# Moving the load of x from SyncE's queue to ScalarE's in a state-space and attention kernel

## The chip, the cores and the metric

The kernel runs on one core of a Trainium2 chip. A core has five engines that work side by side: TensorE (PE, matmuls), VectorE (DVE), ScalarE (ACT), GpSimd (POOL) and SyncE (SP), which here only issues DMAs. Each engine takes its instructions strictly in the order in which they were written, and that includes the instructions that issue DMAs: an instruction that has to wait holds up everything behind it on its engine. The metric is the time of one execution in device microseconds (us). Before the change it is 10996.49 us, the median of three runs (10985.81 to 11037.44).

## The reference

The input is x of 16 images with 128 channels and 64 x 64 pixels, that is 4096 tokens each, in float32. There are two layers.

```python
x = x + mamba(group_norm(x))          # layer 0
t = tokens(x)
t = t + attention(layer_norm(t))      # layer 1
t = t + moe(layer_norm(t))
```

Layer 0 is a selective state-space block: `xz = u @ W_in` gives 256 inner channels and a gate z; a causal convolution of width 4 and a silu follow; a projection gives dt, B and C; and for each of 16 states n the recurrence `h = exp(delta * A_n) * h + delta * u * B_n` runs over the tokens, with `y = sum over n of C_n * h`. Then `y * silu(z)` is projected back with `W_out` and added to x. The attention is a causal running softmax with eight fixed queries (a running maximum, a running sum and a running weighted sum of values). The mixture of experts lets each of 64 experts choose eight tokens, pools them, applies two matrices and adds the result back.

## The kernel before

The kernel has three phases: layer 0 and the attention of layer 1 interleaved (to about 10,150 us, nearly everything); the choice of tokens for the experts; the experts and the last sum. The change touches only the first.

The first phase cuts each image into 8 blocks of L = 512 tokens, 128 blocks in all, with channels on the partitions. The main loop runs over k, the number of the block, and inside it over n, the number of the state, 0 to 15. Everything is put into that double loop by hand: the order of the source is the order on each engine, since every engine is wrapped in `InOrder`, whose one line (L31) is why nearly all rows of the profile bear the line L31. Rows are told apart by the names of their tiles.

In step (k, n) VectorE makes the product `bx` of `du` with B_n (`product`) and runs two scans (`scan`) that give h; POOL multiplies h by C_n into `da` and, for each odd n below 14, issues a DMA that adds the previous state's `da` to this one (`add_pair`); TensorE turns such sums of pairs into PSUM tile `y_ps` (`add_y`). At n = 4 `add_y` takes states 0 and 1. B_n and C_n of a block come to all partitions in one load of tile `bct`, 512 KB, issued by SP in `load_bc` three states ahead, from a small DRAM tile `bcs`. There are five buffers of `bct`, so the load for state n waits until POOL has finished state n - 5.

The rest of the work of several blocks is written between these steps in `beside(n)` and `between(n)`. With m = k - 9 the block that the attention works on, and k + 1 the next block:

- n = 1 to 3: `norm_block` normalises the x of block k + 1 in place (ScalarE). `turn_y` turns the y of block k - 1 back into `yb_ps`, and `gate` (n = 3, VectorE) multiplies it by the gate `z`.
- n = 7: ScalarE stores the attention's split scores to DRAM (`pd<-parts`, `store_parts`).
- n = 8: TensorE projects block k + 1 (`dbl_ps`), and ScalarE stores its B and C (`bcs<-dbl`, `store_bc`).
- n = 9: `gate_silu` of block k: two matmuls `z_ps` read the x tile `xb` of block k, and two silus on ScalarE make `z`. Then come four value matmuls `v_ps` and their silus.
- n = 10: `delta` of block k + 1 (`dt_ps`, softplus on ScalarE), the variance and `rstd` of the attention's next block.
- n = 12, 13: `weights` reads `lh` and `rh` (`w_ps`); `attend` makes `ao_ps`.
- n = 14: VectorE makes the attention's input `xn` from `cen_ps` and `rstd`, right after the product of that state.

The tile `xb` of a block holds its 512 tokens and the three before them, which the convolution needs; the first block of an image has zeros there, put in by a memset on POOL. There are two buffers of `xb`, so the load for block k + 2 overwrites that of block k, whose last readers are the two `z_ps` matmuls of n = 9.

In SP's queue the order around the change, after `load_bc` of state 13 (issued at n = 10), is: the load of `xb` for block k + 2; 16 small loads of 3 KB each that spread `pd` into `lh` and `rh` (`spread_parts`); the load of `bct` for state 14 (issued at n = 11), that for state 15 (n = 12), a load of `xs` from DRAM (`load_x`), and so on.

Of the kernel before, what the change touches and what calls it, by code (L numbers as in the profile page):

```python
# [16 lines left out]
L = 512  # L17
# [22 lines left out]
def conv_attn_hybrid(ctx: ExitStack, tc: tile.TileContext, x, w_in, conv_w, conv_b, w_xproj, w_dt, b_dt,  # L40
# [4 lines left out]
    NBLK = T // L  # L45
# [6 lines left out]
    KC = conv_w.shape[1]  # L52
# [8 lines left out]
    x_f = x.rearrange("b c h w -> b c (h w)")  # L61
# [19 lines left out]
    with ExitStack() as st:  # L81
# [5 lines left out]
        PE, DVE, ACT, POOL, SP = (InOrder(tc, e) for e in (nc.tensor, nc.vector, nc.scalar, nc.gpsimd, nc.sync))  # L87
# [127 lines left out]
        NK = NB * NBLK  # L215
        blocks, gn, res, att = {}, {}, {}, {}

        def load_exp():
            tc.keep_in_program_order(nc.scalar.preload_act_table_set(EXP_LN))
# [4 lines left out]
        def bank(name):  # L224
            return ps.tile([P, L], F32, tag="ps", name=name)
# [13 lines left out]
        def gn_stats(b, i):  # L239
            DVE.bn_stats(gn[b]["stats"][:, i, :], gn[b]["t"])  # L240

        def gn_end(b, part):

            w = gn[b]
            if part == 0:
                w["mv"] = stp.tile([P, 2], F32, tag="mv", name="mv")
                w["gs"] = stp.tile([P, 5], F32, tag="gs", name="gs")
                DVE.bn_aggr(w["mv"], w["stats"].rearrange("p a b -> p (a b)"))
            mv, gs = w["mv"], w["gs"]
            if part == 1:  # L250
                w["gp"] = bank("gn_ps")
                PE.matmul(w["gp"][:, 0:1], gmat, mv[:, 0:1], start=True, stop=True)
                ACT.copy(gs[:, 0:1], w["gp"][:, 0:1])
            if part == 2:
                DVE.tensor_tensor(gs[:, 1:2], mv[:, 0:1], gs[:, 0:1], ALU.subtract)
                DVE.scalar_tensor_tensor(gs[:, 1:2], gs[:, 1:2], gs[:, 1:2], mv[:, 1:2], ALU.mult, ALU.add)
            if part == 3:
                w["gp"] = bank("gn_ps2")
                PE.matmul(w["gp"][:, 0:1], gmat, gs[:, 1:2], start=True, stop=True)
                ACT.activation(gs[:, 2:3], w["gp"][:, 0:1], AF.Ln, bias=eps)  # L260
                ACT.activation(gs[:, 3:4], gs[:, 2:3], AF.Exp, scale=-0.5)
            if part == 4:
                DVE.tensor_scalar(gs[:, 4:5], gs[:, 0:1], gs[:, 3:4], -1.0, ALU.mult, ALU.mult)


        def load_block(k):

            b, i = divmod(k, NBLK)
            t = xbp.tile([P, KC - 1 + L], F32, tag="xb", name="xb")
            if i == 0:  # L270
                POOL.memset(t[:, : KC - 1], 0.0)
                SP.dma_start(t[:, KC - 1 :], x_f[b, :, :L])
            else:
                SP.dma_start(t, x_f[b, :, i * L - (KC - 1) : (i + 1) * L])
            blocks[k] = dict(k=k, b=b, i=i, xb=t)

        def norm_block(k):
            w = blocks[k]
            t, gs = w["xb"], gn[w["b"]]["gs"]
            t = t[:, KC - 1 :] if w["i"] == 0 else t  # L280
            ACT.activation(t, t, AF.Identity, bias=gs[:, 4:5], scale=gs[:, 3:4])
# [14 lines left out]
        def gate_silu(k):  # L296
            w = blocks[k]
            z = w["z"] = m1.tile([P, NH2, L], F32, tag="z", name="z")
            for a in range(NH2):
                pt = bank("z_ps")  # L300
                PE.matmul(pt, wz[:, bass.ts(a, P)], w["xb"][:, KC - 1 :], start=True, stop=True)
                ACT.activation(z[:, a, :], pt, AF.Silu)
# [36 lines left out]
        def load_bc(k, n):  # L339
            w = blocks[k]  # L340
            t = w["bc", n] = bcp.tile([P, 2, L], F32, tag="bc", name="bct")
            SP.dma_start(t, w["bcs"][n : n + N + 1 : N, :].partition_broadcast(P))
# [7 lines left out]
        def product(k, n):  # L350

            w = blocks[k]
            bx = w["bx"] = bps.tile([P, NH2, L], F32, tag="bx", name="bx")
            DVE.tensor_tensor(bx, w["du"], bc(w["bc", n][:, 0:1, :], [P, NH2, L]), ALU.mult)
# [17 lines left out]
        def add_pair(k, n):  # L372

            w = blocks[k]
            POOL.dma_start(w["da", n], w.pop(("da", n - 1)), accum_op=ALU.add)

        def keep_state(k, n):
            w = blocks[k]
            h = w.pop(("h", n))
            if w["i"] < NBLK - 1:  # L380
                POOL.tensor_copy(gn[w["b"]]["state"][:, n, :], h[:, :, L - 1])
# [53 lines left out]
        def store_residual(b, part):  # L435
            SP.dma_start(t1_d[b, :, bass.ts(part, T // 4)], res[b][:, bass.ts(part, T // 4)])
# [15 lines left out]
        def ln_center(m):  # L452
            s = att[m]
            s["cen"] = bank("cen_ps")
            PE.matmul(s["cen"], cmat, s.pop("x"), start=True, stop=True)

        def ln_square(m):
            s = att[m]
            s["sq"] = short("sq")
            ACT.activation(s["sq"], s["cen"], AF.Square)  # L460
# [131 lines left out]
        def value(m, c, g):  # L592
            s = att[m]
            if g == 0:
                s["v", c] = vp_.tile([P, HD, P], F32, tag="v", name="v")
            hs = bass.ts(g, 4)
            vp = ps.tile([P, 4, P], F32, tag="ps", name="v_ps")
            PE.matmul(vp.rearrange("p h d -> p (h d)"), s["xn"][:, bass.ts(c, P)],
                      wv[:, hs, :].rearrange("p h d -> p (h d)"), start=True, stop=True)
            ACT.activation(s["v", c][:, hs, :], vp, AF.Silu)  # L600
# [72 lines left out]
        def decays(k, n, count, lead=LEAD):  # L673

            nonlocal made
            for _ in range(count):
                if made < len(order) and made <= k * N + n + lead and order[made][0] in blocks \
                        and "delta" in blocks[order[made][0]]:
                    decay(*order[made])
                    made += 1  # L680
# [4 lines left out]
        for i in range(2):  # L685
            gn_load(1, i)
            gn_stats(1, i)
        load_block(0)
        load_block(1)
        load_exp()  # L690
        for part in range(5):
            gn_end(0, part)
# [13 lines left out]
        for k in range(NK + LAG + 1):  # L706
            b, i = divmod(k, NBLK)
# [22 lines left out]
            def beside(n):  # L730
# [104 lines left out]
                if n == 9:  # L835
                    if mn is not None:
                        ln_center(mn)
                        ln_square(mn)
                    if cur is not None:
                        gate_silu(cur)  # L840
                    if m is not None:
                        value(m, 1, 0), value(m, 1, 1)
                if n == 10:
# [30 lines left out]
            for n in range(N):  # L874
                if cur is not None:
                    product(cur, n)
                if ends is not None and n == 2:
                    gn_end(ends, 0)
                beside(n)
                if n in (4, 11, 12, 15):  # L880
                    decays(k, n, 2)
                if cur is not None:
                    later = k * N + n + LEAD_BC
                    if later < NK * N:
                        load_bc(*order[later])
                    scan(cur, n, between)
                    keep_state(cur, n)
                    if n % 2 and n < N - 2:
                        add_pair(cur, n)
                else:  # L890
                    between(n)
                if cur is not None and n >= 4 and n % 2 == 0:
                    add_y(cur, n - 3)

                if 8 <= n <= 11 and i == 0 and prev is not None:
                    store_residual(b - 1, n - 8)
                if 14 <= n <= 15 and i == 0 and cur is not None:
                    load_residual(b, n - 14)
                if n < 2 and i == 1 and cur is not None:
                    load_residual(b, n + 2)  # L900
                if n == 7 and mn is not None:
                    load_x(mn, True)
                if n == 8 and stat is not None:
                    gn_load(*stat)
                if n == 10 and k + 2 < NK:
                    load_block(k + 2)
                if n == 10 and m is not None:
                    spread_parts(m)
                if n == 12 and m is not None:
                    load_x(m)  # L910
# [8 lines left out]
    with ExitStack() as st:  # L919
        PE, DVE, ACT, POOL, SP = (InOrder(tc, e) for e in (nc.tensor, nc.vector, nc.scalar, nc.gpsimd, nc.sync))  # L920
# [163 lines left out]
        for it in range(NIT + LATE + 2):  # L1084
            p, i = divmod(it, NBLK)
# [73 lines left out]
    with ExitStack() as st:  # L1159
        ps = st.enter_context(tc.tile_pool(name="cps", bufs=4, space=PSUM))  # L1160
        cp = st.enter_context(tc.tile_pool(name="cp", bufs=2))
        for pr in range(NB // 2):
# [4 lines left out]
            for j in range(2):  # L1167
                b = 2 * pr + j
                t = cp.tile([P, T], F32, tag=f"t{j}", name=f"tc{j}")
# [34 lines left out]
```

## Time and profile before

| | |
|---|---|
| median of three runs | 10996.49 us |
| the profiled execution | 11003.26 us |
| its span | 11001.4 us |
| TensorE busy | 9347.4 us (85%), mean granted clock 0.894 |
| VectorE busy | 8982.2 us (82%) |
| ScalarE busy | 7293.5 us (66%) |
| POOL busy | 7464.0 us (68%) |
| blocks 10 to 126, mean time of one | 76.3 us |
| blocks 0 to 8 (no attention yet), mean time of one | 64.6 us |

A row of the groups reads: line, engine, operation, tile written <- tiles read, shape, count | busy us in all, mean ns of one | idle time of the engine just ahead of these instructions, and what ended it. In the waits, a row reads: the engine and the tile that it was about to write, <- what it waited for, then us in total, times, and the longest. SPq and ACTq are the DMA-issuing instructions of SP and ScalarE. The idle time of an engine costs something only if the work that ends the block hangs on it.

### The profile page before, as it was taken

How to read it: one execution, taken by the hardware profiler on the slowest of the kernel's cores; microseconds unless marked ns; L12 is line 12 of the kernel's file. 1: busy time of each engine (PE TensorE's matmuls, PEld its weight loads, DVE VectorE, ACT ScalarE, POOL GpSimd, SP SyncE). 2: the span in 40 equal slices, each digit the busy share in tenths (PEclk: the TensorE clock that was granted, in tenths of full speed). 3: DMA queues.
4: the chain of work that ended last, by engine and by line, in shares of the span. 5: the costliest groups of instructions: out<-in, count | busy, mean ns of one | idle time of the engine just before them, and what ended most of it. 6: DMA issues, size and time to landing. Idle time of an engine off the chain costs nothing.

```text
span 11001.4 us, 157987 instructions
## 1 busy us (share of the span) xinstructions
PE 9347.4 (85%) x55389; PEld 5527.2 (50%) x55389; DVE 8982.2 (82%) x9987; ACT 7293.5 (66%) x12924; POOL 7464.0 (68%) x4771
## 2 busy tenths in 40 slices
PE   4578888888888889998888888988888888888775
PEld 2345555555555555555555555555545555544652
DVE  8998888888889888888888888888888888830753
ACT  5567677776777767777676776777767777754740
POOL 7887777777777777777777777777777777720000
PEclk7789999999999999999999999999999999999886
DMA  7777777777777777777777777777767777720348
GB/s 191 199 198 180 193 181 193 181 194 180 180 200 180 192 178 195 183 196 179 182 188 179 196 181 192 182 198 183 192 176 182 198 180 189 178 71 29 113 158 336
DMA packets 944361, 1995.67 MB, mean 181 GB/s; under 512 B 103040, under 2 KB 188688, under 8 KB 936400
## 3 DMA queue, kind: packets, MB, share of 16 engines
q1 hardware_dynamic: 751056, 1448.08, 45.0%
q0 software_dynamic: 129024, 469.82, 21.9%
q10 hardware_dynamic: 63488, 67.67, 1.8%
q8 instruction: 440, 7.21, 0.2%
q14 instruction: 353, 2.89, 0.1%
HBM read 1363.98 MB, written 151.52 MB: 138 GB/s over the span
## 4 chain that ended last, share of the span: by engine, by line
PE 53%; ACT 15%; DVE 14%; DMA 9%; issue 6%; SPq 2%; POOL 1%; ACTq 1%; DVEq 0%; POOLq 0%
PE ao_ps L31 9%; PE xs_ps L31 7%; DVE h L31 6%; PE v_ps L31 6%; PE y_ps L31 5%; DMA da<-da 5%; PE k_ps L31 5%; DVE bx L31 4%; PE o_ps L31 4%; ACT da L31 4%; PE carry_ps L31 4%; PE dbl_ps L31 2%; DMA bct<-bcs 2%; ACT wm L31 2%; SPq L31 2%
## 5 line engine op out<-in xcount | busy, mean ns | idle before, releaser
L31 POOL TENSOR_TENSOR da<-h,bct 128x1024 f32<-128x1024 f32 x2048 | 6454.8, 3152 | 2069.6 <-DVE h L31 1635.8
L31 DVE TENSOR_TENSOR_SCAN h<-da,state,bx 128x512 f32<-128x512 f32 x3584 | 4414.5, 1265 | 170.0 <-DVE bx L31 2.9
L31 DVE TENSOR_TENSOR bx<-du,bct 128x1024 f32<-128x1024 f32 x2048 | 2590.6, 1265 | 882.0 <-DMA bct<-bcs 816.3
L31 ACT ACTIVATE da<-delta,a_neg 128x512 f32<-128x512 f32 x4096 | 2629.5, 716 | 107.3 <-DMA da<-da 87.8
L31 PE MATMUL y_ps<-ident,da 128*128 128x128 f32 x9216 | 1415.6, 307 | 381.4 <-DMA da<-da 381.1
L31 PEld LDWEIGHTS y_ps<-ident,da 128*128 128x128 f32 x9216 | 1198.4, 159 | 817.9 <-DMA da<-da 437.8
L31 PE MATMUL ao_ps<-wm,v 128*128 128x128 f32 x8192 | 1259.7, 317 | 239.0 <-ACT wm L31 195.4
L31 PEld LDWEIGHTS ao_ps<-wm,v 128*128 128x128 f32 x8192 | 1186.5, 227 | 503.8 <-ACT wm L31 320.6
L31 PE MATMUL v_ps<-wv,xn 128*128 128x512 f32 x2048 | 1060.3, 640 | 261.1 <-ACT xc L31 241.3
L31 ACT ACTIVATE v<-v_ps 128x512 f32<-128x512 f32 x1024 | 610.1, 597 | 733.0 <-PE v_ps L31 731.1
L31 ACT ACTIVATE wm<-w_ps 128x512 f32<-128x512 f32 x1024 | 552.4, 591 | 708.7 <-PE w_ps L31 707.2
L31 PE MATMUL k_ps<-xn,wk 128*128 128x512 f32 x2048 | 946.7, 596 | 5.6 <-ACT kt L31 5.3
L31 PE MATMUL xs_ps<-xb,wc 128*128 128x512 f32 x2048 | 925.2, 594 | 1.8 <-issue 1.8
L31 POOL DMA_DIRECT2D da<-da x896 | 788.0, 879 | 172.2 <-POOL state L31 98.1
L31 PEld LDWEIGHTS v_ps<-wv,xn 128*128 128x128 f32 x2048 | 346.9, 195 | 784.1 <-issue 301.5
L31 ACT ACTIVATE kt<-k_ps 128x512 f32<-128x512 f32 x1024 | 585.9, 600 | 180.5 <-PE k_ps L31 151.8
L31 DVE TENSOR_TENSOR_SCAN h<-da,bx 128x512 f32<-128x512 f32 x512 | 599.8, 1206 | 25.6 <-ACT da L31 0.5
L31 PEld LDWEIGHTS xs_ps<-xb,wc 128*128 128x128 f32 x2048 | 371.1, 191 | 397.9 <-issue 383.3
L31 ACT ACT_TABLE_LOAD x395 | 506.8, 1283 | 52.0 <-ACT parts L31 46.3
L31 PEld LDWEIGHTS k_ps<-xn,wk 128*128 128x128 f32 x2048 | 371.4, 191 | 328.8 <-issue 254.2
L31 POOL COPY state<-h 128x2 f32<-128x2 f32 x1792 | 461.7, 258 | 0.0
L31 PE MATMUL w_ps<-rh,lh 64*128 64x512 bf16 x1024 | 293.9, 431 | 183.4 <-DMA rh<-pd 83.9
(196 smaller groups left out, 10704.8 us busy)
## 6 DMA issues: line engine op xcount, KB each, us to landing
bct<-bcs SPq DMA_DIRECT2D x2048, 512.0 KB
da<-da POOLq DMA_DIRECT2D x896, 512.0 KB, 7.6
xs<-t_d SPq DMA_DIRECT2D x240, 256.0 KB
xs<-in_x_dram SPq DMA_DIRECT2D x128, 256.0 KB
xt<-in_x_dram SPq DMA_DIRECT2D x64, 512.0 KB
t_d<-xt SPq DMA_DIRECT2D x64, 512.0 KB
t_d<-xs ACTq DMA_DIRECT2D x256, 128.0 KB
t<-t_d SPq DMA_DIRECT2D x128, 256.0 KB
```

The source lines that it names most:

```text
L31: return lambda *args, **kw: self.tc.keep_in_program_order(f(*args, **kw))
```

## The change

`load_block` gets the queue as an argument. The two loads ahead of the loop stay on SP. In the loop the load for block k + 2 is now issued by ScalarE at n = 9, right behind the two silus of `gate_silu` and ahead of the silus of v, instead of by SP at n = 10 behind `load_bc` of state 13 and ahead of the spread loads. The memset of the three columns for the first block of an image, 16 in all, is split off into `no_tokens`; it stays on POOL and goes from n = 10 to n = 13.

```diff
-        def load_block(k):
+        def load_block(k, queue):
 
             b, i = divmod(k, NBLK)
             t = xbp.tile([P, KC - 1 + L], F32, tag="xb", name="xb")
             if i == 0:
-                POOL.memset(t[:, : KC - 1], 0.0)
-                SP.dma_start(t[:, KC - 1 :], x_f[b, :, :L])
+                queue.dma_start(t[:, KC - 1 :], x_f[b, :, :L])
             else:
-                SP.dma_start(t, x_f[b, :, i * L - (KC - 1) : (i + 1) * L])
+                queue.dma_start(t, x_f[b, :, i * L - (KC - 1) : (i + 1) * L])
             blocks[k] = dict(k=k, b=b, i=i, xb=t)
+
+        def no_tokens(k):
+            if k % NBLK == 0:
+                POOL.memset(blocks[k]["xb"][:, : KC - 1], 0.0)
...
-        load_block(0)
-        load_block(1)
+        for k in range(2):
+            load_block(k, SP)
+            no_tokens(k)
...
                     if cur is not None:
                         gate_silu(cur)
+                    if k + 2 < NK:
+                        load_block(k + 2, ACT)
                     if m is not None:
                         value(m, 1, 0), value(m, 1, 1)
...
-                if n == 10 and k + 2 < NK:
-                    load_block(k + 2)
+                if n == 13 and k + 2 < NK:
+                    no_tokens(k + 2)
                 if n == 10 and m is not None:
                     spread_parts(m)
```

## The prediction

> **What bounds the kernel now.** I read the page first, then the waits of the DMA queue of SP, then one block in order of time, then the waits of TensorE over the steady stretch, and last the stretches of one block with their clock.
>
> The page (engine totals, then two groups: busy, mean ns | idle before, releaser):
>
> ```profile
> span 11001.4 us, 157987 instructions
> PE 9347.4 (85%) x55389; PEld 5527.2 (50%) x55389; DVE 8982.2 (82%) x9987; ACT 7293.5 (66%) x12924; POOL 7464.0 (68%) x4771
> ...
> L31 DVE TENSOR_TENSOR bx<-du,bct 128x1024 f32<-128x1024 f32 x2048 | 2590.6, 1265 | 882.0 <-DMA bct<-bcs 816.3
> ...
> L31 PE MATMUL y_ps<-ident,da 128*128 128x128 f32 x9216 | 1415.6, 307 | 381.4 <-DMA da<-da 381.1
> ```
>
> VectorE loses 816 us to loads of B and C (`bct`). The waits of SP's queue (waited for: us, times, longest) say which wait in front of those loads is not simply a full buffer:
>
> ```profile
> SPq L31 <- POOL state L31: 4850.8, 1218, 8.3
> SPq L31 <- POOL da L31: 1456.0, 308, 8.2
> SPq L31 <- PE z_ps L31: 1063.1, 118, 12.8
> ```
>
> The POOL rows are free buffers being awaited, well ahead of need. The z_ps row is the load of x: 118 times 9.0 us. One block in order of time (start, duration; four lines of SP's queue, the third of them the first of 16 spread loads, then one of VectorE):
>
> ```profile
> 5019.47 0.36 SPq L31 DMA_DIRECT2D bct<-bcs  x1
> 5029.72 0.35 SPq L31 DMA_DIRECT2D xb<-in_x_dram  x1
> 5030.15 0.27 SPq L31 DMA_DIRECT2D lh<-pd  x1
> ...
> 5036.94 0.89 SPq L31 DMA_DIRECT2D bct<-bcs  x2
> 5042.63 1.23 DVE L31 TENSOR_TENSOR bx<-du,bct 128x1024 f32<-128x1024 f32 x1 [7.42 <-DMA bct<-bcs]
> ```
>
> SP stands from 5019.8 to 5029.7 behind the x load, which waits for the gate's matmuls (`z_ps`) to stop reading the buffer; then come 16 small loads (`lh`, `rh`), and the load for state n=14 is issued at 5036.94 and in use 5.7 us later. Over blocks 12 to 123 the trace gives a mean idle of 6.65 us ahead of n=14 and 0.03 to 0.22 ahead of the other fifteen.
>
> Does that idle set the end? TensorE's waits between 1000 and 9500 us (8500 / 76.3 = 111 blocks of 76.3 us):
>
> ```profile
> PE v_ps L31 <- ACT xc L31: 227.0, 111, 2.3
> PE ao_ps L31 <- ACT wm L31: 150.6, 236, 1.1
> PE y_ps L31 <- DMA da<-da: 100.8, 75, 3.4
> PE dt_ps L31 <- ACT delta L31: 86.4, 111, 0.8
> PE o_ps L31 <- ACT wm L31: 82.4, 111, 1.0
> PE w_ps L31 <- ACT rstd L31: 64.2, 78, 2.1
> PE et_ps L31 <- ACT parts L31: 53.1, 111, 0.9
> PE w_ps L31 <- DMA rh<-pd: 52.0, 29, 3.6
> ```
>
> This limits the gain. TensorE is busy 67.9 us of a 76.3 us block and idle 8.4; most of the idle is ScalarE answering TensorE, which this change doesn't touch. Only two rows hang on VectorE or on SP's queue: the y_ps wait at n=4 for the added pair of states 0 and 1 (100.8 / 111 = 0.91 us a block) and the wait for `rh` (52.0 / 111 = 0.47). So TensorE with ScalarE is the bound by itself, and VectorE's stall is mostly its slack against TensorE.
>
> **The change part by part.**
>
> *Removed: the z_ps wait in SP's queue.* What is late next? The 16 spread loads then stand first. They need `pd`, stored by ScalarE at 5018.17 in this block. The packets of ScalarE's queue show its last byte 6.0 us after the issue (5% 2.9, 95% 6.3), so 5024.2. [...] There the twelfth spread load waits for ScalarE's store of B and C (`bcs`, issued at 5025.51, last packet 2.4 us later: 5027.9). From the first spread load to the n=14 load takes 5036.94 - 5030.15 = 6.8 us, so that load goes out at 5024.2 + 6.8 = 5031.0; the twelfth is due near 5028.5, after 5027.9, so `bcs` adds nothing. Gain 5.9 us. It lands 5.7 later, 5036.7; VectorE's natural time is 5031.39 + 3.84 = 5035.2. Its stall on `bct` falls from 7.4 to about 1.5 us.
>
> *Where the stall goes.* Right after the product of n=14 VectorE does `xn`, which needs ScalarE's `rstd`, ended at 5038.8 here; it began `xn` at 5043.77. So VectorE comes 5.0 us earlier against TensorE, not 5.9. That lead lasts until the gate at n=3, which needs `yb_ps`: that slack is 0.9 us in the mean and zero in a quarter of the blocks, so the gate takes the lead back. The add of states 0 and 1 is started before it, hence 4 to 5 us earlier; the longest y_ps wait is 3.4 us, so this wait goes. The `rh` wait goes too, the spread ending some 5.9 us earlier.
>
> *Worth of it.* By subtraction: 0.91 + 0.47 = 1.4 us a block. By the blocks of the trace that already had no y_ps wait: 32 of 112 average 75.45 us against 76.33 for all, 0.9 less, and runs of such blocks in a row (39 to 43) take 75.2. I take 1.1. The z_ps row counts 118 blocks: 118 x 1.1 = 130 us. The first nine blocks run at 64.6 us without the stall, and the ten steps after the last block and the later phases have none: nothing there.
>
> *Added: one DMA issue on ScalarE per block, 126 in all.* Its nearest row is `pd` or `bcs`, 0.33 us. After the second gate silu ScalarE idles 0.36 us for `v_ps` (5030.32 to 5030.68), and the next silu of v has 0.26 more. So 0 to 0.1 us a block is seen; I take 0.05, 6 us in all. Without that cover it is 0.36 x 126 = 45 us, since softplus and the matmuls of delta are queued behind it. The new queue also has waits: the x load waits for its predecessor on its semaphore, the fifth spread load, and the `bcs` store now waits for the load of n=13 (before: n=10). Fifth spread load: issued near 5025.5, a small load is down within 2.6 us (in the old queue the ninth, which waits for the first, goes out at 5032.80 after 5030.15), so 5028.1, against 5030.3 when ScalarE gets there: hidden with 2 us to spare, under 1 us in blocks where `pd` is late. Load of n=13: issued at 5019.47, in use 5 to 5.7 us later in the n=14 row, so 5025.2 against 5025.51: hidden with almost nothing to spare. Bounds: 0, and 0.5 us a block (59 us). I take 0, because a VectorE that runs early issues n=13 early.
>
> *Removed from SP: 126 issues of 0.35 us*, inside the same wait. *Moved: the memset of the first three columns*, 16 of 0.09 us on POOL, later on a queue that waits for VectorE 1650 us: nothing. The landing of x is needed about a quarter block later (norm at n=1): nothing.
>
> [...] The z_ps row shows what moves here is a wait at the head of an in-order queue, 9.0 us; so I go by the row. [...]
>
> ```profile
> 5036.00:5039.40 3.40, 2.69 (x12) 1.00 (x11) 0.00 (x0) 3.34 (x6) 2.70 (x3) 0.50 0.24 73
> 5039.40:5042.80 3.40, 2.93 (x13) 2.53 (x14) 0.17 (x1) 3.40 (x7) 0.00 (x0) 0.50 0.62 143
> ```
>
> (stretch, busy us of PE, PEld, DVE, ACT, POOL, then the granted clock.) It is at half for 12.8 us a block, and over the blocks each such microsecond costs 0.41 us. [...] But blocks without a y_ps wait have 12.6 us of it: TensorE's half clock begins at the ScalarE waits around `dt_ps`. I count none of it.
>
> Sum: 11001.4 - 130 + 6 = 10,877 for the span. The profiled execution took 11003.26, 6.8 above the median 10996.49, and 1.9 lies around the span: 10,877 + 1.9 - 6.8 = 10,872. I say 10,870.
>
> **The rivals.**
> - *Hidden anyway.* TensorE's 76.3 us stays because phases shift and ScalarE's small new waits take the 1.1 back. For: a quarter of the blocks have `bcs` and n=13 within a microsecond of each other. Time 10,990.
> - *The clock comes up too.* Two windows of 3.4 us less at half: 6.8 x 0.41 = 2.8 us a block more, 118 x 2.8 = 330: 10,540. For: blocks with 6.8 us of half clock exist. Against: most of those had long y_ps waits.
> - *VectorE was the bound.* All 6.65 us return: 118 x 6.65 = 785: 10,212. Against: TensorE's idle.
> - *Slower: ScalarE waits for the spread.* If the fifth spread load lands after 5030.3, ScalarE stands in order before v, softplus and delta, and every late microsecond beyond 0.36 is TensorE's. Parity at 1.1 + 0.36 = 1.5 us of mean lateness, and 0.5% slower at 1.9; at 2.4 us the net is -0.9 a block: 11,100. Needs `pd` some 4 us later than its packets show.
> - *Not done as written*: excluded; the built program has the x load on ScalarE right behind the gate's silus.
>
> **How the numbers follow.** Forecast 0.67 (own range 10,800 to 10,935); hidden 0.15; clock 0.09; VectorE 0.03; slower 0.06. The range 10,780 to 11,000 leaves out the clock, VectorE and slower cases, 0.18. About half a per cent (10,941 to 11,051) is what a measurement here can tell from no change. Faster: 0.67 less 0.02, plus 0.12 = 0.77; same 0.15 + 0.02 = 0.17; slower 0.06.
>
> **What would show it.** Right: no z_ps row in SP's waits; bct idle of VectorE under 300 us, its wait for `rstd` and `yb_ps` up by several hundred together; y_ps wait between 1000 and 9500 near zero; TensorE idle near 7 us of a 75.2 us block. Wrong: ScalarE rows that wait for `lh`, `rh` or `bct`; half clock far from 12.8 us; a block above 76.

## The result and the profile after

The changed kernel takes 10930.35 us in the median of seven runs (10917.17 to 10944.61); the kernel before, in seven runs beside it, 11012.28 us (10985.81 to 11055.86). The ratio is 0.9917, with a 95% interval of 0.9894 to 0.9939: 0.8% faster. The forecast was 10,870, about 60 us less. Set against the 10996.49 us from which it was worked out, it is a ratio of 0.9885; by the ratios a gain of 1.15% was forecast and 0.83% came.

The page of the changed kernel (engine totals, then three groups):

```profile
span 10929.5 us, 157776 instructions
PE 9405.6 (86%) x55389; PEld 5549.3 (51%) x55389; DVE 9012.1 (82%) x9987; ACT 7284.5 (67%) x12924; POOL 7530.3 (69%) x4771
...
L31 DVE TENSOR_TENSOR bx<-du,bct 128x1024 f32<-128x1024 f32 x2048 | 2598.3, 1269 | 470.3 <-DMA bct<-bcs 404.1
...
L31 PE MATMUL y_ps<-ident,da 128*128 128x128 f32 x9216 | 1428.1, 309 | 279.2 <-DMA da<-da 278.9
...
L31 DVE TENSOR_TENSOR z<-yb_ps,z 128x512 f32<-128x512 f32 x256 | 164.8, 685 | 339.7 <-PE yb_ps L31 339.3
```

VectorE's wait for `bct` has halved, from 816.3 to 404.1 us. But it stands 339.3 us in front of the gate instead, where the kernel before has

```profile
L31 DVE TENSOR_TENSOR z<-yb_ps,z 128x512 f32<-128x512 f32 x256 | 164.2, 683 | 32.0 <-PE yb_ps L31 31.5
```

And TensorE's busy time has risen by 58.2 us, from 9347.4 to 9405.6, with the same 55389 matmuls. Its mean granted clock is 0.890; before it was 0.894.

The waits of SP's queue:

```profile
SPq L31 <- POOL state L31: 5192.8, 1275, 9.8
SPq L31 <- POOL da L31: 1705.8, 388, 8.3
SPq L31 <- DMA pd<-parts: 905.3, 112, 44.4
...
SPq L31 <- PE z_ps L31: 2.6, 14, 0.2
```

The wait on `z_ps` is down from 1063.1 to 2.6 us. The row on `pd` has grown in its place, from 353.9 us in 10 waits: the spread loads now reach the head of the queue before the store that they read. One block in order of time: two loads of `bct` (states 12 and 13, the second issued at 5062.56), the first spread load, the load of state 14, and the product of state 14 on VectorE:

```profile
5058.75 4.17 SPq L31 DMA_DIRECT2D bct<-bcs  x2
5068.14 0.26 SPq L31 DMA_DIRECT2D lh<-pd  x1
...
5074.77 0.89 SPq L31 DMA_DIRECT2D bct<-bcs  x2
5081.28 1.23 DVE L31 TENSOR_TENSOR bx<-du,bct 128x1024 f32<-128x1024 f32 x1 [2.97 <-DMA bct<-bcs]
```

The store of `pd` was issued at 5061.55, so the first spread load follows it by 6.6 us (6.67 in the mean). The load of state 14 is issued 6.6 us after that (7.34 in the mean) and in use 6.5 us later (6.4). Over blocks 12 to 123 the idle time ahead of state 14 falls from 6.65 to 3.29 us.

TensorE's waits between 1000 and 9500 us, the stretch shown before:

```profile
PE v_ps L31 <- ACT xc L31: 228.7, 112, 2.3
PE ao_ps L31 <- ACT wm L31: 226.2, 328, 0.9
PE dt_ps L31 <- ACT delta L31: 87.1, 112, 0.8
PE o_ps L31 <- ACT wm L31: 83.3, 112, 1.0
PE w_ps L31 <- ACT rstd L31: 68.2, 111, 1.4
...
PE var_ps L31 <- ACT v L31: 19.2, 32, 2.3
...
PE y_ps L31 <- DMA da<-da: 9.7, 9, 1.8
```

The wait for added pairs (100.8) is all but gone, and that for `rh` (52.0) has left the list. Against that, `ao_ps` waiting for ScalarE's `wm` has grown from 150.6 to 226.2. Over blocks 12 to 123 that is 0.68 us a block, 0.48 of it in the attention's second half, right behind the y_ps wait: that wait had covered it. TensorE now comes there earlier and finds ScalarE not ready. The wait of `var_ps` for the silu `v`, 19.2 us, is new. So are two waits of ScalarE, in the same stretch, for transfers that it does not use:

```profile
ACT v L31 <- DMA bct<-bcs: 30.7, 17, 2.1
ACT v L31 <- DMA lh<-pd: 26.2, 20, 2.8
```

What this is worth, measured from gate to gate (from the end of a block's last `z_ps` matmul, the fourth in the trace, which has each of the two of the source as two, to that of the next block) over blocks 12 to 123:

| mean of a block, us | before | after | difference |
|---|---|---|---|
| period | 76.33 | 75.79 | -0.54 |
| TensorE idle | 8.44 | 7.42 | -1.02 |
| TensorE busy | 67.89 | 68.38 | +0.49 |
| of it with the clock at half | 12.77 | 13.53 | +0.76 |

Over the execution: the gate of block 9 ends at 678.6 us before and 675.4 after; the 118 periods from there to block 127 take 76.27 and 75.71 us, 66.3 us in all; the tail after it 1323.1 and 1320.8. That is 3.2 + 66.3 + 2.3 = 71.8, all but rounding of the 71.9 us between the two spans.

### The profile page after: what moved, and what is told of

It is laid out like the page before. It is cut to its first block, busy times and chain, and to the rows that moved or that the text cites. A ratio compares the mean times of both kernels' runs of the same rounds, so it can differ in the third digit from the quotient of the medians.

```text
span 10929.5 us, 157776 instructions
## 1 busy us (share of the span) xinstructions
PE 9405.6 (86%) x55389; PEld 5549.3 (51%) x55389; DVE 9012.1 (82%) x9987; ACT 7284.5 (67%) x12924; POOL 7530.3 (69%) x4771
## 4 chain that ended last, share of the span: by engine, by line
PE 61%; ACT 18%; DVE 7%; DMA 7%; issue 5%; SPq 1%; ACTq 1%; POOL 1%; DVEq 0%; POOLq 0%
PE ao_ps L31 10%; PE k_ps L31 8%; PE v_ps L31 7%; PE xs_ps L31 7%; PE y_ps L31 6%; ACT da L31 5%; PE carry_ps L31 4%; PE o_ps L31 4%; DVE h L31 3%; PE s_ps L31 3%; ACT L219 3%; ACT wm L31 2%; PE dt_ps L31 2%; DVE bx L31 2%; PE dbl_ps L31 2%
## 5 line engine op out<-in xcount | busy, mean ns | idle before, releaser
L31 DVE TENSOR_TENSOR bx<-du,bct 128x1024 f32<-128x1024 f32 x2048 | 2598.3, 1269 | 470.3 <-DMA bct<-bcs 404.1
L31 PE MATMUL v_ps<-wv,xn 128*128 128x512 f32 x2048 | 1035.8, 629 | 257.0 <-ACT xc L31 240.9
L31 POOL COPY state<-h 128x2 f32<-128x2 f32 x1792 | 509.0, 284 | 0.0
L31 DVE TENSOR_TENSOR z<-yb_ps,z 128x512 f32<-128x512 f32 x256 | 164.8, 685 | 339.7 <-PE yb_ps L31 339.3
```

What stands on the lines that cost most here:

```text
L31: return lambda *args, **kw: self.tc.keep_in_program_order(f(*args, **kw))
```

## The experiments

Each kernel is the changed one with one edit, unless the diff says otherwise. Ratios are to the kernel before on the same chip; periods, idle and half-clock time are means of a block from the one profiled execution, as in the table above.

**Is it the second queue, or only the wait that leaves the spread's front?** The load of x goes back to SP, but behind the load of state 15.

```diff
-                    if k + 2 < NK:
-                        load_block(k + 2, ACT)
...
+                if n == 12 and k + 2 < NK:
+                    load_block(k + 2, SP)
                 if n == 13 and k + 2 < NK:
```

> The changed kernel, but the load of x goes back to SP, behind the load of B and C for state 15 (n = 12) and not in front of the spread loads. If the gain comes only from taking the z_ps wait out from in front of the state 14 load, the queue doesn't matter: VectorE's idle ahead of n = 14 stays near 3.3 us (before: 6.65) and the time is that of the changed kernel, 10,930, or up to 0.3 us a block (30 us) less, since ScalarE no longer waits for the fifth spread load: 10,900 to 10,930. Rival, that a second queue is what helps (issue time, or both queues at work side by side): back to 10,990 to 11,010.

Measured: 10884.65 us (10877.62 to 10900.52), ratio 0.9892 [0.9875, 0.9909]. ScalarE's queue isn't needed: the version with the load of x on SP is at least as fast. Its runs do not overlap those of the changed kernel (lowest 10910.31 of 13), though the two ratio intervals do. TensorE's idle time is the same in both, 7.38 against 7.42; the difference of 0.42 us in the period (75.37) is TensorE busy for 67.99 us instead of 68.38, with 12.77 us at half clock instead of 13.53. So the place behind the gate's silus on ScalarE costs time, and the cost shows in TensorE's busy time, most of it as clock (by estimate 0.31 us, at the prediction's 0.41 us for each of the 0.76 at half clock), and not as idle. (The expectation had 10,900 to 10,930; the gain was larger.)

**Does the new DMA in front of v delay TensorE?** The load stays on ScalarE, but behind the silus of v.

```diff
-                    if k + 2 < NK:
-                        load_block(k + 2, ACT)
                     if m is not None:
                         value(m, 1, 0), value(m, 1, 1)
+                    if k + 2 < NK:
+                        load_block(k + 2, ACT)
```

> The changed kernel, but the load of x stands on ScalarE behind the two silus of v that follow the gate's silus, some 2 us later. The profile of the changed kernel has ScalarE's load of x over 0.3 us late in a quarter of the blocks and a new wait of TensorE, var_ps for the silu of v, of 0.18 us a block. If that wait for the fifth spread load costs time, var_ps goes to zero and the time falls by 10 to 30 us to 10,900 to 10,920; if it is slack, 10,930.

Measured: 10921.98 us (10900.6 to 10942.33), 0.9924 [0.9905, 0.9943]: as the changed kernel. TensorE's `var_ps` wait (19.2) falls to 0, and its `dt_ps` wait rises from 87.1 to 112.2: the same lateness, now a wait of ScalarE for `rh` (27.2 us in 20 waits), hits what is next in ScalarE's order, softplus. Half clock is 13.65 us. Moving the issue within ScalarE's queue moves its cost and doesn't remove it.

**Is VectorE the bound after all?** The spread loads go behind the load of state 14, so that this is early.

```diff
-                if n == 10 and m is not None:
+                if n == 11 and m is not None:
                     spread_parts(m)
```

> The changed kernel, but the 16 spread loads stand behind the load of B and C for state 14 (n = 11). VectorE's idle ahead of n = 14 goes to 0.1 us, so a VectorE-bound kernel gains 3.2 us a block: 10,550. TensorE-bound: no gain from that. But in the built program ScalarE's store of B and C (bcs) then waits, for its completion semaphore, for the load of state 14 to land, near 3 us after its natural time; if waits of that kind on ScalarE are TensorE's, the wait is paid in part: 1 to 3 us a block slower than the changed kernel, 11,050 to 11,280; if they are slack, 10,930.

Measured: 11190.97 us (11175.88 to 11206.5), 1.0168 [1.0147, 1.019]. The stall ahead of state 14 is gone (0.03 us), and the kernel is 2.5% slower than the changed one (1.0168 / 0.9917): period 78.12, TensorE idle 9.25. Removing VectorE's stall alone is therefore not worth its size: VectorE now waits 479.3 us for `yb_ps` (309.1 in the changed kernel) and 491.4 for `rstd` (10.5). What costs the time is on ScalarE (waits of ScalarE, then of TensorE, 1000 to 9500 us):

```profile
ACT v L31 <- DMA bct<-bcs: 277.3, 69, 7.8
```
```profile
PE z_ps L31 <- ACT v L31: 147.1, 89, 5.4
```

ScalarE has no business with `bct`. What waits is its store of `bcs`, just ahead of this silu in its queue. One block of ScalarE, in which the load of state 14 was issued at 5042.98 and the store could go out only 5.5 us later (the copy that makes `dbl`, its store, and the next silu, which waited 4.41 us behind the store):

```profile
5043.83 0.58 ACT L31 COPY dbl<-dbl_ps 40x512 f32<-40x512 f32 x1 [1.24 <-PE dbl_ps L31]
...
5048.45 0.32 ACTq L31 DMA_DIRECT2D bcs<-dbl  x1
5048.82 0.60 ACT L31 ACTIVATE v<-v_ps 128x512 f32<-128x512 f32 x1 [4.41 <-DMA bct<-bcs]
```

That the spread itself comes later is not the reason: TensorE's list has no wait for `lh` or `rh`. In the changed kernel the same store waits for the load of state 13, as foreseen; these are the 30.7 us (17 waits) above, and the 26.2 us (20 waits) are the load of x waiting for the fifth spread load. In the changed kernel's block shown above, the load of state 13 had landed at 5068.85 and the store of `bcs` went out at 5068.93; the fifth spread load, issued at 5070.69, had landed at 5072.35 and the load of x went out at 5072.37. In the trace's records each of these two pairs names one completion semaphore.

**Is TensorE the bound?** The changed kernel with less work on TensorE: the matmuls that add x to the attention's output are left out, so the output lacks that residual.

```diff
                         attend_before(mp_, 1)
-                        add_x(mp_, 0)
...
                         attend_before(mp_, 3)
-                        add_x(mp_, 1)
```

> The changed kernel without the four short matmuls a block that add the attention's own input to its output (add_x, both halves); the output lacks that residual. In the profile each half takes 0.43 us of TensorE at full clock, 0.86 us a block in all, and VectorE, POOL and SP do exactly what they did. If TensorE sets the block: 0.8 to 1 us a block faster, 118 x 0.9 = 106 us, 10,825 (ratio about 0.982). If VectorE or the loads set it: 10,930.

Measured: 10893.59 us (10887.61 to 10897.85), 0.9888 [0.9871, 0.9906]. TensorE is busy 0.96 us a block less (67.42), but the period falls by 0.28 (75.51): idle grows from 7.42 to 8.1. TensorE's work is thus not all that counts. ScalarE's waits, in the same stretch:

```profile
ACT v L31 <- DMA lh<-pd: 90.8, 59, 4.3
...
ACT v L31 <- DMA bct<-bcs: 72.2, 36, 3.0
```

These waits of ScalarE for transfers that it does not use have risen from 26.2 and 30.7, and TensorE's wait for `v` at `var_ps` from 19.2 to 66.7. As TensorE gets ahead, ScalarE more often reaches its DMAs before the transfers that they wait for have landed: 59 and 36 times, where it was 20 and 17 in the changed kernel.

**Has VectorE slack now?** The changed kernel with the product of state 13 made twice.

```diff
-            DVE.tensor_tensor(bx, w["du"], bc(...), ALU.mult)
+            for _ in range(2 if n == 13 else 1):
+                DVE.tensor_tensor(bx, w["du"], bc(...), ALU.mult)
```

> The changed kernel with the product of state 13 made twice on VectorE, 1.25 us more for VectorE in every block. If TensorE with ScalarE sets the block and VectorE only waits (2.8 us at the gate, 3.3 us at n = 14), the time stays within 0.3 us a block: 10,930 to 10,965, and the gate's wait falls by about 1.2 us. If VectorE is the bound: 128 x 1.25 = 160 us more, 11,090.

Measured: 10977.59 us in 15 runs (10963.13 to 10989.95), 0.9971 [0.9962, 0.9981], that is 47 us slower than the changed kernel. The second product is dearer than the 1.25 us of the expectation: VectorE's busy time rises by 391 us, from 9012.1 to

```profile
PE 9408.2 (86%) x55389; PEld 5542.9 (51%) x55389; DVE 9403.0 (86%) x10115; ACT 7286.2 (66%) x12924; POOL 7684.7 (70%) x4771
```

In the trace the second product takes 3.24 us in the mean (blocks 12 to 123); why is not known. In the profiled execution (span +31.9) the gate of block 9 ends 34.8 us later, the steady period is only 0.09 us longer (75.88), and the tail is 13.6 shorter. So the loss lies in the first nine blocks, which have no attention: they lose some 3.9 us each, and VectorE is busy 3.7 us longer in each, so VectorE sets their time, or nearly. In the steady stretch it is busy 3.1 us a block longer and has the time: its waits take that up.

```profile
DVE z L31 <- PE yb_ps L31: 273.0, 108, 5.3
DVE bx L31 <- DMA bct<-bcs: 89.9, 46, 5.5
```

In the changed kernel these rows are 309.1 and 385.8.

**Do ScalarE's waits for transfers that it does not use cost anything once x is back on SP?** To the version with x behind state 15, the store of `bcs` from SP is added, ahead of the spread; ScalarE then issues fewer DMAs.

```diff
-            ACT.dma_start(w["bcs"], w["dbl"][R:, :])
+            (queue or ACT).dma_start(w["bcs"], w["dbl"][R:, :])
...
-                        store_bc(nxt)
...
+                if n == 10 and nxt is not None:
+                    store_bc(nxt, SP)
```

> The kernel with the load of x late on SP, and besides the store of B and C (bcs) taken off ScalarE and put on SP between the load for state 13 and the spread loads, so that ScalarE no longer waits for the load of state 13 to land (48 us, 25 times, in the late-SP kernel's waits of ScalarE between 1000 and 9500 us). If that wait is TensorE's: 20 to 50 us faster than the late-SP kernel, 10,835 to 10,865. If it is slack, or if the spread loads, now behind the bcs store, cost as much: 10,885.

Measured: 10889.39 us (10876.24 to 10894.83), 0.9883 [0.9865, 0.9901]; half clock 12.86 us. No difference from x behind state 15 alone. With TensorE's full work these waits do not set the time there.

The same, again without the attention's residual:

> The kernel in which SP issues both the load of x (late) and the store of B and C, again without the four matmuls a block that add the attention's own input to its output (the output lacks that residual). Taking them out of the changed kernel gave only 0.29 us of the 0.86 us a block, while ScalarE's waits for the spread loads (lh) rose from 26 to 91 us and for the loads of B and C from 31 to 72 us. If those semaphore waits on ScalarE are the second limit, they are gone here and TensorE's 0.86 us come back: 0.7 to 0.9 us a block under the kernel with both on SP, 10,785 to 10,810. If something else (VectorE's chain, a queue) is the second limit: 10,855, as little as there.

Measured: 10816.73 us (10812.75 to 10852.65), 0.9827 [0.9808, 0.9847]: 73 us under the kernel just told, where the same removal gave 29 to 37 us in the changed kernel (to its medians of 10922.05 and 10930.35). ScalarE has no waits for `lh` or `bct` left there. It points to those waits of ScalarE as the second limit behind TensorE. By the ratios it is 0.56% against 0.29%, and the intervals do not separate the two, so this is suggested and not shown.

**The changed kernel once more**, beside these.

> The changed kernel once more, on the same chip as the three others, for the comparison with the kernel whose load is late on SP: 10,930, ratio 0.992. Against 10,885 for the late-SP kernel: if the difference of 45 us is ScalarE's new waits, it stays in a second set of runs.

Measured: 10922.05 us (10910.31 to 10934.99), 0.9914 [0.9899, 0.993], period 75.80, half clock 13.41. The rise of the half clock is not an accident of one profile: with the load of x on ScalarE it is 13.53, 13.65 and 13.41 us a block (the changed kernel, the one with the load behind v, and the changed kernel again), on SP 12.77, 12.77 and 12.86 (before, x behind state 15, and that with `bcs` on SP). The granted clock of all executions agrees: 0.892 in the mean of 13 of the changed kernel and 0.890 of six with the load behind v, against 0.894 of five with x behind state 15 and of four with `bcs` on SP too. It does not hold for every kernel: without the attention's residual the half clock is 13.35 us with the load on ScalarE and 13.59 on SP (the slowest of its four runs), and the mean clock 0.890 in both.

**What is the clock worth?** To the version with x behind state 15, nine matmuls of 128 x 128 x 256 whose result nothing uses are added in TensorE's gaps: three and two behind the two matmuls of delta, two ahead of and two behind the first weights.

```diff
+        def fill(m, count):
+            for _ in range(count if "o" in gn else 0):
+                PE.matmul(gn["o"][:, L // 2 :], wv[:, 0, :], att[m]["xn"][:, : L // 2],
+                          start=True, stop=True, skip_group_check=True)
...
                 softplus(d[:, a, :], pt, bdt[:, a : a + 1])
+                if m is not None:
+                    fill(m, 3 - a)
...
+                        fill(m, 2)
                         weights(m, 0)
+                        fill(m, 2)
```

> The kernel with the load of x late on SP, with nine dense matmuls of 128 x 128 by 256 columns added a block, whose result nobody reads, in TensorE's gaps after the gate (three and two behind the two delta matmuls, two and two around the first weights). They cost 9 x 0.22 = 2 us of TensorE at full clock, partly inside gaps. If the half clock (12.8 us a block, 0.41 to 0.49 us lost for each) is set by how dense TensorE's work is there, it falls by two windows or more, 6.8 x 0.45 = 3 us, and the kernel gains up to 1 to 2 us a block: 10,650 to 10,800. If not, it pays for the matmuls: 10,950 to 11,130, with the half clock unchanged.

Measured: 10736.51 us (10720.24 to 10751.54), 0.9747 [0.9725, 0.9769]: the fastest kernel of this study, 1.5% under the version without the fill (0.9747 / 0.9892). The stretch from 1000 to 9000 us (busy us and count of PE, PEld, DVE, ACT, POOL; granted clock; DMA share; GB/s), first of the version without the fill, then of the filled one:

```profile
1000.00:9000.00 8000.00, 7217.22 (x42399) 4208.28 (x42399) 7114.57 (x7060) 5729.49 (x10026) 6252.97 (x3932) 0.92 0.73 189
```
```profile
1000.00:9000.00 8000.00, 7293.79 (x45010) 4293.52 (x45009) 7241.57 (x7176) 5827.30 (x10186) 6360.17 (x3999) 0.98 0.74 192
```

Half clock falls from 12.77 to 2.22 us a block. The fills occupy 4.85 us of TensorE (the expectation had 2), and all other matmuls fall from 67.99 to 63.55: 4.44 us for 10.55 us, or 0.42 us of work per microsecond of half clock, which agrees with the 0.41 of the prediction. Of the 4.44 us only 1.28 reach the period (74.09): TensorE stands without its own work for 74.09 - 63.55 = 10.5 us, part of it filled, where it stood 7.4.

Fewer of them, three between the matmuls of delta and two ahead of the weights:

> The kernel with the load of x late on SP and five of the nine added matmuls, three between the two delta matmuls and two ahead of the first weights. The nine took the half clock from 12.8 to 2.3 us a block and TensorE's busy time from 68.0 to 67.6 us although they add 2 us themselves. If the gaps between the delta matmuls and ahead of the weights are what starts the half clock, five keep it below 4 us and the kernel gains the 0.9 us of the four left out: 10,630 to 10,740. If the stretch behind the weights decides, the half clock comes back to 7 to 10 us: 10,800 to 10,870.

Measured: 10867.61 us (10859.16 to 10878.29), 0.987 [0.9853, 0.9886]. Half clock is down to 5.46 us, yet the period only to 75.24, and the ratio's interval overlaps that of the version without fills. The half clock lies between the two cases of the expectation, the time in the slower one. The clock came up and most of the time didn't follow; TensorE's wait of `ao_ps` for `wm`, about 12 us after the gate, grew from 0.53 to 1.84 us a block. A higher clock by itself was little gain here: the matmuls saved must be ones that something waits for.

The nine fills in the kernel before, and in the changed one:

> The kernel before the change with the nine added matmuls of the filled kernel (which has the load of x late on SP and ratio 0.9747). Without them the step from the kernel before to the one with the late load was worth 0.9892. If the two gains simply add, this has 0.9747 / 0.9892 = 0.985, 10,850. If VectorE's 6.65 us stall behind the z_ps wait is only just covered by TensorE at its present pace, a faster TensorE uncovers it, TensorE's y_ps wait rises above the 0.9 us a block of the kernel before, and less of the fill's gain is seen: 0.988 to 1.0, 10,880 to 11,010.

> The changed kernel with the nine added matmuls. If the load of x on ScalarE is free, it has the ratio of the filled kernel with the late load on SP less the 0.3% between their bases: 0.977, 10,760. If ScalarE's wait for the fifth spread load is a limit close behind TensorE (as in the run with less TensorE work, where the wait for lh rose to 91 us), a faster TensorE runs into it: 0.981 to 0.990, 10,800 to 10,900, and ScalarE's wait for lh or rh goes above 90 us between 1000 and 9500 us.

Measured: before with fills 11061.92 us (11025.89 to 11105.3), 1.0048 [1.003, 1.0066]; changed with fills 10776.75 us (10774.47 to 10808.24), 0.9795 [0.9768, 0.9822]. The same fill makes the kernel before slower, though its half clock falls to 4.6 us, and the others 1.2 and 1.5% faster. If the gains had added, the kernel before would have had 0.985; it missed that, and the milder case of the expectation too. Before, with fills, TensorE meets VectorE's stall (waits of TensorE, then of VectorE, 1000 to 9500 us):

```profile
PE y_ps L31 <- DMA da<-da: 165.5, 97, 4.3
```
```profile
DVE bx L31 <- DMA bct<-bcs: 832.4, 132, 13.1
...
DVE z L31 <- PE yb_ps L31: 5.7, 6, 2.2
```

The y_ps wait goes from 100.8 to 165.5, and VectorE waits for TensorE at the gate only 5.7 us in all (17.0 without fills): VectorE with its stall now sets the block. So the stall was covered by TensorE's slow clock, and only just. Why it has grown, from 770.6 to 832.4 us, was not followed up. In the changed kernel with fills ScalarE's wait for `lh` stays at 31.9 us, far from the 90 of the expectation's second case; its ratio lies between the two cases. Among filled kernels the change is worth 1 - 0.9795 / 1.0048 = 2.5%, and x behind state 15 on SP 1 - 0.9747 / 1.0048 = 3.0%, against 0.8% and 1.1% without fills.

## Why the prediction was right or wrong

**The z_ps wait leaves SP's queue, and the spread comes next: right in kind, 2 us short.** The wait is gone but for 2.6 us, and `pd` is what is late. Relative to the gate's last matmul the load of state 14 is issued 3.18 instead of 7.10 us after, 3.9 us earlier and not 5.9. Its terms were each a little low: from store to first spread load 6.67 us (6.0 was taken, from the last packet), from there to the load 7.34 (6.8), from issue to use 6.4 (5.7). So the stall stayed at 3.29 us (1.5), and VectorE's wait for `bct` at 404.1 us, above the bound of 300 that the prediction gave.

**The gate takes the lead back: right.** VectorE's wait for `yb_ps` between 1000 and 9500 us rises from 17.0 to 309.1 us; that for `rstd` stays small, 10.5.

**Worth of it, 1.1 us a block: right in its two rows, and close in the sum by some luck.** The waits for the added pair and for `rh` went away, even with the smaller lead, and TensorE's idle fell by 1.02 us. But terms that were not counted made up for each other: `ao_ps` for `wm` grew by 75.6 us between 1000 and 9500 us and `var_ps` by 19.2, while `ao_ps` for VectorE's x went from 34.4 to 3.9 and `w_ps` for `da` from 18 to 0.

**The half clock, "I count none of it": this is the term that was mis-sized.** Predicted time unchanged at 12.8 us a block; measured 13.53, and TensorE busy 0.49 us longer. Over 118 blocks that is 58 us, and the span's gain fell 52 us short of the forecast (72 instead of 124). At the 0.41 us of the prediction, the 0.76 us explain 0.31 of the 0.49. The prediction asked only whether less idle time would give some half clock back; that it could grow stood among the signs of being wrong and not in the sum. That it is back at 12.77 us with x behind state 15 shows that the rise in sum goes with the load on ScalarE and not with the smaller stall. That it equals the kernel before is chance: there 9.90 us of it lie in the first 40 us after the gate and 2.86 later, in the version with x behind state 15 11.43 and 1.34.

**The cost on ScalarE, bounds 0 and 59 us, taken as 0: mis-sized, and the same 0.4 us a block.** The version with x on SP is 46 us faster than the changed kernel (37 against the second set of runs; some 25 us by the ratios). It does not appear as TensorE idle, and so is not a further cost beside the half clock. The step that failed is "hidden with 2 us to spare". The prediction had the fifth spread load issued 4.2 us ahead of the gate's last matmul (5025.5 against 5029.7). Measured, it is 2.0 us in the mean: the first spread load goes out 4.2 us ahead and not 5.5, and the fifth 2.1 us behind it and not 1.3. In 29 of blocks 12 to 123 the load of x goes out more than 0.93 us after the gate, that is over 0.3 us after the second gate silu; it then follows the fifth spread load, for which it waits, by 2.3 us.

| mean of a block | 29 late blocks | the other 83 |
|---|---|---|
| first silu of v after the gate, changed kernel | 1.81 us | 1.05 us |
| the same, x behind state 15 | 0.99 us | 0.99 us |
| period, changed kernel | 76.64 us | 75.50 us |
| the same blocks, x behind state 15 | 75.62 us | 75.28 us |
| half clock, changed kernel | 14.36 us | 13.24 us |
| the same blocks, x behind state 15 | 12.71 us | 12.79 us |

So a quarter of the blocks carries 1.02 x 29 / 112 = 0.26 of the 0.42 us (0.30 of 0.43 in the second profile of the changed kernel, with 33 such blocks), and much of the longer half clock. These blocks were picked by their lateness and not set by an edit, so this points to the wait for the fifth spread load without proving it; what the other blocks lose stays open. The issue of the DMA itself is hidden, as foreseen: where the load is not late, the first silu of v starts at 0.99 us (median) in both.

**The rivals.** That the gain is hidden in full did not come true, but some two fifths of it are gone (52 of 124 us of span), mostly for that rival's reason, small new waits on ScalarE. VectorE as the bound (10,212) is refuted for the changed kernel by the doubled product: VectorE was held 3.1 us longer a block, and the steady blocks took that for 0.09 us. The stall removed at a loss agrees. In the kernel before with fills VectorE and its stall do come to set the block. That the clock comes up too (10,540) did not happen here; the filled kernels show that it would have been worth something, but for 10.5 us of it only 1.28 us a block came through. The slower case, ScalarE standing behind transfers that are not its own, did occur in the change, in a quarter of the blocks: in the mean of all blocks the first silu of v is 0.26 us late, far from the 1.1 us that make parity (the 1.5 less the 0.36 that are hidden). In the kernel with state 14 first it made the change a loss, through waits of the same kind (277.3 us for `bct`). Of the prediction's signs of being wrong, ScalarE rows for `lh` and `bct` came up (26.2 and 30.7 us), and the half clock moved; the block stayed under 76 us.

## What to carry to other kernels

A stall of one engine is worth the waits of the bounding engine that hang on it. Made from the bounding engine's own rows, that sum was 1.4 us here, 1.1 were taken, and idle fell by 1.02, when the stall itself was 6.65 us; new waits behind the old ones took the rest. When a wait is taken from the head of an in-order queue, first try to put it later in the same queue: on ScalarE's queue the load of x held that engine's compute here behind a transfer that it does not use (26.2 us for `lh`), and that kernel was 46 us slower than the one with the load later in SP's queue (37 against the second set of runs). A change can be worth three times as much once another limit is lifted (0.8% against 2.5% here), so a limit that lies just under the bound is worth a test in combination before it is called slack.

## What the runs showed of the hardware

- TensorE's half clock set in without a long idle. In blocks 12 to 123 of the changed kernel TensorE is idle 10% of the time and its longest idle gap is 2.3 us; yet the clock is at half for 13.53 us of 75.79, mostly in pieces of 3.4, 10.2 or 13.7 us. Some 4.9 us a block of matmuls put into TensorE's gaps reduce the half clock to 4.6 us in the kernel before, and to 2.22 and 2.74 in the two faster versions.
- The half clock's price is alike by two ways: 0.41 us per microsecond from the spread over blocks, and 0.38 to 0.43 from the four filled kernels, each against the same kernel without fills (0.42 for the fastest).
- ScalarE was held by transfers that it neither issues nor uses: 277.3 us of its time went to `bct` (69 waits, the longest 7.8 us), in a kernel made 2.5% slower by a change in the order of DMAs on SP.
